# A transformer block with mixture of experts: the last block's rows reach the last four tiles through products instead of a store and gathers

## The chip, the core and the metric

The kernel runs on one core of a Trainium2 chip. The metric is device time in microseconds of one execution, start to end, as the median of several runs. Engine names are those of the profile: PE is TensorE (PEld its weight loads), DVE is VectorE, ACT is ScalarE, POOL is GpSimd, SP is SyncE, which here only issues DMAs.

## The reference

The input is `x` of 32 sequences x 256 steps x 256 features, with one condition vector per sequence. Two layers follow each other:

```python
x = x + attn(cond(x, cond_1024))       # gated input, causal attention of one head over 256 steps
x = x + ffn(cond2(x, cond_1024))       # low-rank conditioned layer, then the block below
```

`ffn` attends over the first axis, of 32, with the 256 steps as its batch (16 heads over 4 key groups), and ends in a mixture of experts over all 8192 tokens:

```python
logits = ln2(h1) @ router_weight                       # 8 experts
top_p, top_i = top_k(softmax(logits), 2)               # 2 experts a token, weights sum to 1
# tokens sorted by expert, at most cap = 2560 a expert; later ones are dropped
fc1 = gelu(einsum('ech,ehf->ecf', xt, moe_w1))         # 256 -> 512
fc2 = einsum('ecf,efh->ech', fc1, moe_w2)              # 512 -> 256
out = h1 + scatter_add(token, fc2 * prob)              # both experts' rows, weighted, back at the token
```

The change lies in the last line: how the experts' rows come back to their tokens. All data are float32.

## The kernel before

**Stages.** By the profile's time the first layer runs up to about 370 us, the attention of the second layer up to about 700 us, and the experts from there to the end. The change is in the last third.

**Experts by blocks.** The (token, expert) pairs are laid out in slots: 256 slots a block, each block of one expert. Block `n` takes four steps. `gather(n)` (L736) brings the 256 tokens' rows from DRAM with two indirect DMAs on POOL's queue. `turn_in(n)` (L753) transposes them on PE and scales them on DVE. `weights(n)` (L744) copies the expert's weights on DVE (L748). `hidden(n)` (L765) and `result(n)` (L778) are the two products on PE, 16 of 128x256 each, with GELU and a copy out of PSUM on ACT. `result` then stores the block's 256 rows to `y_d` in DRAM, from SP.

**Slots of a token.** The routing puts into `yrow[:, j, k]` the slot of each of the 128 tokens of tile `j` (there are 64 tiles, 16 groups of four) for its k-th expert, and into `prob[:, j, k]` its weight, zero where the pair was dropped. Routing is complete before block 20, called `AHEAD`.

**How many blocks.** The number of blocks depends on the data. Three variants of the code from block 20 on are in the program, for 54, 62 and 74 blocks, and a register picks one (`arm`, L1680 on). These inputs take the first, of 54: the profile has 108 gathers `xx<-z_d`, two a block.

**Back to the tokens.** In `experts` (L1617), tile by tile: `fetch_rows(j)` issues two indirect DMAs on POOL's queue (L1633), which gather from `y_d` the rows of the tile's tokens for k = 0 and 1, and for the first tile of a group one load `rs<-res_d` on SP (L1627), the residual rows of the whole group. `combine(j)` does `ot = yg*prob + rs` and `ot = yg*prob + ot` on DVE (L1644), and after the fourth tile stores the group's 512 KB with four DMAs on SP (L1650).

**When a tile may be fetched.** The pairs were laid out so that the slots of early tiles lie in early blocks. `ready[g]` is the number of blocks that must be in `y_d` before group `g` may be gathered; with 54 blocks it is 22, 24, 26, ... 49 (group 13), 51 (group 14), 54 (group 15). In each block from 20 on the loop fetches up to two tiles that are ready, and combines them two blocks later. Group 15, the tiles 60 to 63, needs all 54 blocks, so it is fetched after the loop: first all four `fetch_rows`, then the combines of tiles 58 to 63.

**What sets the order.** The experts' part is under a manual schedule: each engine runs its instructions in the order in which they are written, and so does each engine's DMA queue. An instruction that waits holds up all that is written behind it for the same engine.

Of the kernel before, what the change touches and what calls it, by code (L numbers as in the profile page):

```python
# [9 lines left out]
F32 = mybir.dt.float32  # L10
I32 = mybir.dt.int32
BF16 = mybir.dt.bfloat16
AF = mybir.ActivationFunctionType
ALU = mybir.AluOpType
AX = mybir.AxisListType
PSUM = bass.MemoryType.PSUM
DRAM = bass.MemoryType.DRAM

P = 128
S = 32  # L20
T = 256
D = 256
# [4 lines left out]
NJ = NTOK // P  # L27
NSG = NJ // 4
CAP = int(math.ceil(NTOK * 2 / NE * 1.25))
BLK = 256  # L30
# [7 lines left out]
AHEAD = 20  # L38
# [11 lines left out]
def block_kernel(ctx: ExitStack, tc: tile.TileContext, a: dict, out: bass.AP):  # L50
# [14 lines left out]
    nc = tc.nc  # L65
# [9 lines left out]
    ident = const.tile([P, P], F32, name="ident")  # L75
# [41 lines left out]
    with ExitStack() as c1:  # L117
# [40 lines left out]
        def load_c2w2(f):  # L158
# [7 lines left out]
            out=fac.rearrange("s f o -> s (f o)"), in_=a["c2_b2"].to_broadcast([S, 2 * RANK * D])  # L166
# [9 lines left out]
        base = k1.tile([P, 2, DR], F32, name="base")  # L176
        nc.sync.dma_start(
            out=base[:, :, :D], in_=a["base"].rearrange("(c p) o -> p c o", p=P)
# [13 lines left out]
        for blk in (0, 2):  # L192
            nc.gpsimd.affine_select(
                out=cmask[:, blk, :], in_=cmask[:, blk, :], compare_op=ALU.is_ge,
# [299 lines left out]
        def low_rank(s):  # L494
# [44 lines left out]
            scale_g, pattern=[[1, NSG]], base=1, channel_multiplier=0,  # L539
            allow_small_or_imprecise_dtypes=True,  # L540
# [4 lines left out]
            rev, pattern=[[-1, NE]], base=NE, channel_multiplier=0,  # L545
            allow_small_or_imprecise_dtypes=True,
# [26 lines left out]
        for b in range(4):  # L573
            q = slice(32 * b, 32 * b + 32)
            nc.gpsimd.affine_select(
                out=lows[q], in_=lows[q], compare_op=ALU.is_gt, fill=0.0, base=0,
                pattern=[[0, 4], [1, S]], channel_multiplier=-1,
# [5 lines left out]
            out=lowp, in_=ones, compare_op=ALU.is_gt, fill=0.0, base=0,  # L583
            pattern=[[1, P]], channel_multiplier=-1,
# [4 lines left out]
            icolf, pattern=[[1, P], [0, 8]], base=0, channel_multiplier=0,  # L589
            allow_small_or_imprecise_dtypes=True,  # L590
# [8 lines left out]
            irowf, pattern=[[1, 2 * NB]], base=0, channel_multiplier=0,  # L599
            allow_small_or_imprecise_dtypes=True,  # L600
# [16 lines left out]
        for i in range(2):  # L617
# [4 lines left out]
            prow, pattern=[[0, 1]], base=0, channel_multiplier=1,  # L622
            allow_small_or_imprecise_dtypes=True,
# [22 lines left out]
        for q in range(3):  # L646
            for b in range(4):
                r = SURE * (4 * q + b)
                nc.sync.dma_start(
                    out=rowbitsc[r : r + SURE],  # L650
                    in_=rowbits[32 * b : 32 * b + SURE, PACK * q : PACK * (q + 1)],
# [11 lines left out]
        for b in range(4):  # L663
            q = slice(32 * b, 32 * b + 32)
            for vb in vbd:
                nc.vector.memset(vb[q, :, b, HD:], 1.0)
            nc.gpsimd.affine_select(
                out=tmask[q], in_=tmask[q], compare_op=ALU.is_ge, fill=NEG, base=0,
                pattern=[[0, 2], [-1, S]], channel_multiplier=1,
# [43 lines left out]
    prob = keep.tile([P, NJ, 2], F32, name="prob")  # L713
    gap = keep.tile([P, NJ], F32, name="gap")
    yrow = keep.tile([P, NJ, 2], I32, name="yrow")
# [13 lines left out]
    hts = [ep.tile([P, 4, BLK], F32, name=f"ht{i}") for i in range(2)]  # L729
    yss = [ep.tile([P, 2, D], F32, name=f"ys{i}") for i in range(2)]  # L730
# [3 lines left out]
    xgs, wcs = [], []  # L734

    def gather(n):  # L736
        for h in range(2):
            nc.gpsimd.indirect_dma_start(  # L738
                out=xgs[n % 4][:, h, :], out_offset=None,
                in_=z2_d[: 3 * PACK * P, :] if n < EARLYB else z2_d[:, :],  # L740
                in_offset=bass.IndirectOffsetOnAxis(ap=src_row[:, n, h : h + 1], axis=0),
            )
# [35 lines left out]
    def result(n, ps):  # L778
        we2 = wcs[n % 2][:, 1].rearrange("p (c d) -> p c d", c=4)
        for h in range(2):  # L780
            for f in range(4):
                nc.tensor.matmul(  # L782
                    ps[:, h, :], lhsT=hts[n % 2][:, f, h * P : (h + 1) * P],
                    rhs=we2[:, f, :], start=(f == 0), stop=(f == 3),
                )
        nc.scalar.copy(yss[n % 2], ps)  # L786
        nc.sync.dma_start(
            out=y_d[BLK * n : BLK * (n + 1), :].rearrange("(p h) d -> p h d", h=2),
            in_=yss[n % 2],
        )  # L790
# [529 lines left out]
    out_v = out.rearrange("s (j b) d -> b s j d", b=4)  # L1320
# [3 lines left out]
    p_ys = [pc.tile([P, 2, D], F32, name=f"ps_y{i}") for i in range(2)]  # L1324
    with tc.tile_pool(name="rt", bufs=1) as rt, tc.tile_pool(
        name="rw", bufs=4
# [287 lines left out]
    order.close()  # L1614


    def experts(count, ready, w3):  # L1617

        groups = [{} for _ in range(NSG)]

        def fetch_rows(j):

            g, i = j // 4, j % 4
            v = groups[g]
            if i == 0:
                v["rs"] = w3.tile([P, 4, D], F32, name="rs")
                nc.sync.dma_start(  # L1627
                    out=v["rs"].rearrange("p j d -> p (j d)"), in_=res_d[g]
                )
            upto = ready[g] * BLK  # L1630
            for k in range(2):
                yg = v[i, k] = w3.tile([P, D], F32, name=f"yg{k}", bufs=8)
                nc.gpsimd.indirect_dma_start(  # L1633
                    out=yg, out_offset=None, in_=y_d[:upto, :],
                    in_offset=bass.IndirectOffsetOnAxis(ap=yrow[:, j, k : k + 1], axis=0),
                )

        def combine(j):
            g, i = j // 4, j % 4
            v = groups[g]  # L1640
            if i == 0:
                v["ot"] = w3.tile([P, 4, D], F32, name="ot")
            for k in range(2):
                nc.vector.scalar_tensor_tensor(  # L1644
                    v["ot"][:, i, :], v[i, k], prob[:, j, k : k + 1],
                    v["rs"][:, i, :] if k == 0 else v["ot"][:, i, :], ALU.mult, ALU.add,
                )
            if i == 3:
                for b in range(4):
                    nc.sync.dma_start(  # L1650
                        out=out_v[b, :, 4 * g : 4 * g + 4, :],
                        in_=v["ot"][32 * b : 32 * b + 32],
                    )


        fetched, due = 0, []
        for n in range(AHEAD, count):
            if n + 3 < count:
                gather(n + 3)
            for f2 in range(2):  # L1660
                hidden(n, f2, p_hs[f2])
            if n + 1 < count:
                turn_in(n + 1, p_x)
                weights(n + 1)
            result(n, p_ys[n % 2])
            while due and due[0][0] <= n:
                combine(due.pop(0)[1])
            for _ in range(2):
                if fetched < NJ and ready[fetched // 4] <= n:
                    fetch_rows(fetched)  # L1670
                    due.append((n + 2, fetched))
                    fetched += 1
        while due or fetched < NJ:
            while fetched < NJ and len(due) < 8:
                fetch_rows(fetched)
                due.append((0, fetched))
                fetched += 1
            combine(due.pop(0)[1])

    def arm(count, ready):  # L1680
        with tc.tile_pool(name="w3", bufs=2) as w3, tc.manual_schedule():
            experts(count, ready, w3)

    which = nc.values_load(plan[0:1, 0:1], min_val=0, max_val=len(PLANS) - 1)
    with ExitStack() as elses:
# [60 lines left out]
```

## Time and profile before

| | us |
|---|---|
| runs | 1166.71, 1166.76, 1170.42 |
| median | 1166.76 |
| profiled execution's own time | 1165.57 |
| its span, first to last instruction | 1163.8 |

| engine | busy us | share |
|---|---|---|
| PE | 1075.2 | 92% |
| DVE | 704.8 | 61% |
| POOL | 531.0 | 46% |
| ACT | 392.4 | 34% |

The own time lies 1.8 us over the span. Times inside the profile are us from the span's start. In the profile's lines, `yg<-y_d,yrow` names what is written and what is read, `x4` is a count, and a bracket `[3.62 <-DVE ot L1644]` gives the engine's idle time before the line and what the profile believes ended it. Lines with `SPq` are DMA issues; their time is the issue's, not the transfer's.

### The profile page before, as it was taken

The numbers are of one execution on the slowest core, as the hardware profiler recorded it, in microseconds if no ns is written. First come the engines' busy times: TensorE is split into PE (matmuls) and PEld (weight loads), VectorE is DVE, ScalarE is ACT, GpSimd is POOL, SyncE is SP. The second block draws the span as 40 slices with busy tenths as digits, with TensorE's granted clock in tenths as the row PEclk, the third lists the DMA queues.
The fourth block names the chain that finished last, engine by engine and source line by source line (L and its number), as shares of the span: only waits on it lengthen the run. The fifth ranks groups of instructions, "written<-read, shape, count | busy, mean of one in ns | idle before, by whom it ended". The sixth has DMA issues, their size and how long they took to land.

```text
span 1163.8 us, 17054 instructions
## 1 busy us (share of the span) xinstructions
PE 1075.2 (92%) x5724; PEld 866.3 (74%) x5724; DVE 704.8 (61%) x1784; ACT 392.4 (34%) x942; POOL 531.0 (46%) x781
## 2 busy tenths in 40 slices
PE   8999999999994999999998869997999999999891
PEld 5576888888872777777776648885888888787771
DVE  3554555555561888888888975986222455445452
ACT  2222333333332566666664313210222222222220
POOL 2022222222222466566665545203332777777774
PEclk9999999999997999999999959997999999999996
DMA  9452333333164134254352114101221566665655
GB/s 316 115 148 93 109 114 116 114 115 116 66 155 125 39 111 166 96 182 160 135 180 78 39 64 145 55 37 47 81 73 52 185 203 205 183 204 178 205 182 155
DMA packets 86192, 149.51 MB, mean 128 GB/s; under 512 B 11544, under 2 KB 52144, under 8 KB 85552
## 3 DMA queue, kind: packets, MB, share of 16 engines
q1 hardware_dynamic: 70160, 100.02, 26.5%
q0 software_dynamic: 15936, 48.32, 13.5%
q8 instruction: 47, 0.77, 0.3%
q14 instruction: 49, 0.40, 0.1%
HBM read 90.96 MB, written 57.22 MB: 127 GB/s over the span
## 4 chain that ended last, share of the span: by engine, by line
PE 72%; issue 9%; DMA 8%; DVE 7%; POOL 3%; ACT 1%; SPq 0%; DVEq 0%; POOLq 0%; ACTq 0%
PE ps_y L782 10%; PE ps_h L770 9%; PE p_qkv L858 6%; PE p L502 5%; PE p_z L385 5%; PE p_v L398 5%; PE p_pr L963 4%; PE p_av L929 4%; DMA yg<-y_d,yrow 4%; DMA xx<-z_d,src_row 3%; PE p_sc L888 3%; PE ps_t L917 3%; PE p_s L438 2%; PE p_o L471 2%; PE p_l L413 2%
## 5 line engine op out<-in xcount | busy, mean ns | idle before, releaser
L770 PE MATMUL ps_h<-xt,xx 128*128 128x256 f32 x864 | 197.6, 382 | 0.8 <-DVE xt L760 0.8
L782 PE MATMUL ps_y<-xx,ht 128*128 128x256 f32 x864 | 197.3, 382 | 0.0
L738 POOL DMA_INDIRECT xx<-z_d,src_row x108 | 124.3, 1151 | 149.7 <-issue 78.8
L770 PEld LDWEIGHTS ps_h<-xt,xx 128*128 128x128 f32 x864 | 164.8, 191 | 24.0 <-DVE xt L760 1.2
L782 PEld LDWEIGHTS ps_y<-xx,ht 128*128 128x128 f32 x864 | 161.4, 192 | 20.6 <-ACT ht L774 0.3
L760 DVE TENSOR_SCALAR xt<-ps_xt,ln 128x256 f32<-128x256 f32 x106 | 52.8, 540 | 196.0 <-PE ps_xt L756 196.0
L1633 POOL DMA_INDIRECT yg<-y_d,yrow x128 | 132.1, 1032 | 55.9 <-issue 39.4
L95 POOL TENSOR_SCALAR ve<-mv 128x2 f32<-128x2 f32 (+2 forms) x49 | 10.8, 219 | 237.4 <-DVE mv L103 236.3
L774 ACT ACTIVATE ht<-ps_h 128x512 f32<-128x512 f32 x108 | 64.5, 597 | 136.0 <-PE ps_h L770 134.8
L786 ACT COPY ys<-ps_y 128x512 f32<-128x512 f32 x54 | 31.7, 586 | 213.0 <-PE ps_y L782 182.6
L858 PE MATMUL p_qkv<-wqkv,lnt 128*128 128x384 f32 x256 | 94.7, 494 | 0.0
L908 POOL TENSOR_TENSOR sc<-sc,mx 128x512 f32<-128x512 f32 x64 | 67.9, 1060 | 53.4 <-DVE mx L907 47.5
L929 PEld LDWEIGHTS p_av<-vbd,pt 128*128 128x128 f32 x512 | 68.0, 196 | 27.4 <-ACT pt L922 13.1
L868 ACT COPY vbd<-p_qkv 32x64 f32<-32x64 f32 x256 | 52.7, 206 | 90.2 <-DVE qk L864 87.9
L929 PE MATMUL p_av<-vbd,pt 128*128 128x68 f32 x512 | 67.0, 275 | 8.1 <-ACT pt L922 5.9
L963 PE MATMUL p_pr<-wp,ao 128*128 128x264 f32 x256 | 73.3, 410 | 0.0
L385 PE MATMUL p_z<-yt,m_qk 128*128 128x256 f32 x256 | 68.9, 396 | 0.8 <-ACT yt L370 0.8
L968 POOL TENSOR_TENSOR res<-h,xx 128x256 f32<-128x256 f32 x64 | 43.8, 684 | 54.6 <-DVE h L967 54.4
L748 DVE COPY xx<-wall 128x2048 f32 x54 | 67.4, 1249 | 1.7 <-DMA xx<-z_d,src_row 1.4
L502 PE MATMUL p<-layer,x1t 128*128 128x264 f32 x256 | 66.1, 402 | 2.1 <-ACT x1t L492 1.5
L398 PE MATMUL p_v<-w_vo,yt 128*128 128x256 f32 x256 | 60.6, 379 | 0.0
L502 PEld LDWEIGHTS p<-layer,x1t 128*128 128x128 f32 x256 | 47.1, 194 | 15.7 <-ACT x1t L492 7.4
(302 smaller groups left out, 1874.0 us busy)
## 6 DMA issues: line engine op xcount, KB each, us to landing
xx_d<-o POOLq DMA_DIRECT2D x32, 530.0 KB, 3.5
y_d<-ys SPq DMA_DIRECT2D x54, 256.0 KB
xx<-xx_d SPq DMA_DIRECT2D x13, 1060.0 KB
xt<-in_x_t_dram SPq DMA_DIRECT2D x32, 256.0 KB
xs<-in_x_dram SPq DMA_DIRECT2D x32, 256.0 KB
wall<-in_moe_w_dram SPq DMA_DIRECT2D x16, 512.0 KB
z_d<-h SPq DMA_DIRECT2D x16, 512.0 KB
res_d<-res SPq DMA_DIRECT2D x16, 512.0 KB
```

The costliest lines, as they stand in the source:

```text
L385: nc.tensor.matmul(p_z[:, m, :], lhsT=m_qk[:, c, m * P : (m + 1) * P], rhs=yt[:, c, :], start=(c == 0), stop=(c == 1),)
L398: nc.tensor.matmul(p_v[:, t, :], lhsT=yt[:, c, t * P : (t + 1) * P], rhs=w_vo[:, c, :], start=(c == 0), stop=(c == 1),)
L502: nc.tensor.matmul(p_2, lhsT=v["x1t"][:, c, t * P : (t + 1) * P], rhs=v["layer"][:, c, :], start=(c == 0), stop=(c == 1),)
L738: nc.gpsimd.indirect_dma_start(out=xgs[n % 4][:, h, :], out_offset=None, in_=z2_d[: 3 * PACK * P, :] if n < EARLYB else z2_d[:, :], in_off ...
L748: nc.vector.tensor_copy(wcs[n % 2].rearrange("p a f -> p (a f)"), wall[:, bass.ds(e, 1), :, :].rearrange("p e a f -> p (e a f)"),)
L770: nc.tensor.matmul(ps[:, i, :], lhsT=we1[:, c, f * P : (f + 1) * P], rhs=xts[n % 2][:, c, :], start=(c == 0), stop=(c == 1),)
L782: nc.tensor.matmul(ps[:, h, :], lhsT=hts[n % 2][:, f, h * P : (h + 1) * P], rhs=we2[:, f, :], start=(f == 0), stop=(f == 3),)
L858: nc.tensor.matmul(ps, lhsT=live2[n // 4]["lnt"][:, c, j * P : (j + 1) * P], rhs=wqkv[:, c, :], start=(c == 0), stop=(c == 1),)
L908: nc.gpsimd.tensor_tensor(sc, sc, mx.unsqueeze(2).to_broadcast([P, 16, S]), ALU.subtract)
L929: nc.tensor.matmul(p_a[:, g // 2, :, g % 2, :], lhsT=v["pt"][:, g, :], rhs=vbd[n % 5][:, g], start=True, stop=True,)
L963: nc.tensor.matmul(p_p, lhsT=tiles[n]["ao"][:, gp, :], rhs=wp2[:, gp, :], start=(gp == 0), stop=(gp == 1),)
L1633: nc.gpsimd.indirect_dma_start(out=yg, out_offset=None, in_=y_d[:upto, :], in_offset=bass.IndirectOffsetOnAxis(ap=yrow[:, j, k : k + 1], a ...
```

## The change

For the variants where group 14 is ready before the last block (54 and 62 blocks; not 74), the last block's rows are not stored and not gathered. Group 15 waits for 53 blocks only. For its four tiles:

- Setup, once, ahead of block 20's work: an iota on POOL that numbers the 256 slots of the last block, a float copy of `yrow`, weights `prob_l` that are zero where the slot lies in the last block, and `yrow_l`, the slot clipped to the last row before that block.
- `mark(i)`, in blocks 20 to 23: three DVE instructions make a matrix of 128 tokens x 256 slots, with the weight where the token's slot is, and zero elsewhere.
- `turn_marks(i)`, in blocks 21 to 24: two transposes on PE and a copy on ACT turn it into `own`, slots by tokens.
- `result_alone`, in place of the last `result`: the same 16 products, copied out of PSUM by halves; then eight products of 128x256, `own` by the block's rows, into `p_own`. No store to `y_d`.
- `fetch_rows` of group 15 moves into the loop, at the last block, behind the combines that are due there; from block 51 on up to four tiles are fetched in a block, so that tiles 56 to 59 are all fetched at 51 and combined at 53.
- `combine` of group 15 has a third DVE instruction a tile, which adds `p_own`; its stores go out after every second tile, 64 KB each, alternately from SP and ACT.

```diff
@@ -1614,9 +1614,71 @@
     order.close()
 
 
-    def experts(count, ready, w3):
+    def experts(count, ready, w3, w3p):
+
+
 
         groups = [{} for _ in range(NSG)]
+        last, end = count - 1, NJ - 4
+        alone = w3p is not None
+        if alone:
+            assert ready[NSG - 2] <= last
+            ready = [*ready[:-1], last]
+            own = w3.tile([P, 2, 4, P], F32, name="own", bufs=1)
+            pos = w3.tile([P, 2, P], F32, name="pos", bufs=1)
+            nc.gpsimd.iota(
+                pos, pattern=[[1, 2], [2, P]], base=last * BLK, channel_multiplier=0,
+                allow_small_or_imprecise_dtypes=True,
+            )
+            at_row = w3.tile([P, 4, 2], F32, name="at_row", bufs=1)
+            nc.vector.tensor_copy(at_row, yrow[:, end:, :])
+
+            prob_l = w3.tile([P, 4, 2], F32, name="prob_l", bufs=1)
+            nc.vector.scalar_tensor_tensor(
+                prob_l, at_row, float(last * BLK), prob[:, end:, :], ALU.is_lt, ALU.mult
+            )
+            yrow_l = w3.tile([P, 4, 2], I32, name="yrow_l", bufs=1)
+            nc.vector.tensor_scalar(yrow_l, at_row, float(last * BLK - 1), None, ALU.min)
+            marks = {}
+
+        def mark(i):
+
+            ms = []
+            for k in range(2):
+                m = w3.tile([P, 2, P], F32, name=f"mark{k}")
+                nc.vector.tensor_scalar(
+                    m, pos, at_row[:, i, k : k + 1], prob[:, end + i, k : k + 1],
+                    ALU.is_equal, ALU.mult,
+                )
+                ms.append(m)
+            nc.vector.tensor_tensor(ms[0], *ms, ALU.add)
+            marks[i] = ms[0]
+
+        def turn_marks(i):
+            ps = w3p.tile([P, 2, P], F32, name="p_mark")
+            for h in range(2):
+                nc.tensor.transpose(ps[:, h, :], marks[i][:, h, :], ident)
+            nc.scalar.copy(own[:, :, i, :], ps)
+
+        def result_alone():
+            n = last
+            ps, we2 = p_ys[n % 2], wcs[n % 2][:, 1].rearrange("p (c d) -> p c d", c=4)
+            ys = yss[n % 2]
+            for h in range(2):
+                for f in range(4):
+                    nc.tensor.matmul(
+                        ps[:, h, :], lhsT=hts[n % 2][:, f, h * P : (h + 1) * P],
+                        rhs=we2[:, f, :], start=(f == 0), stop=(f == 3),
+                    )
+                nc.scalar.copy(ys[:, h, :], ps[:, h, :])
+            p_own = w3p.tile([P, 4, D], F32, name="p_own")
+            for i in range(4):
+                for h in range(2):
+                    nc.tensor.matmul(
+                        p_own[:, i, :], lhsT=own[:, h, i, :], rhs=ys[:, h, :],
+                        start=(h == 0), stop=(h == 1),
+                    )
+            return p_own
 
         def fetch_rows(j):
 
@@ -1632,7 +1694,11 @@
                 yg = v[i, k] = w3.tile([P, D], F32, name=f"yg{k}", bufs=8)
                 nc.gpsimd.indirect_dma_start(
                     out=yg, out_offset=None, in_=y_d[:upto, :],
-                    in_offset=bass.IndirectOffsetOnAxis(ap=yrow[:, j, k : k + 1], axis=0),
+                    in_offset=bass.IndirectOffsetOnAxis(
+                        ap=yrow_l[:, i, k : k + 1] if alone and j >= end
+                        else yrow[:, j, k : k + 1],
+                        axis=0,
+                    ),
                 )
 
         def combine(j):
@@ -1641,15 +1707,22 @@
             if i == 0:
                 v["ot"] = w3.tile([P, 4, D], F32, name="ot")
             for k in range(2):
+                w = prob_l[:, i] if alone and j >= end else prob[:, j]
                 nc.vector.scalar_tensor_tensor(
-                    v["ot"][:, i, :], v[i, k], prob[:, j, k : k + 1],
+                    v["ot"][:, i, :], v[i, k], w[:, k : k + 1],
                     v["rs"][:, i, :] if k == 0 else v["ot"][:, i, :], ALU.mult, ALU.add,
                 )
-            if i == 3:
+            n = 4
+            if alone and j >= end:
+                nc.vector.tensor_tensor(
+                    v["ot"][:, i, :], p_own[:, i, :], v["ot"][:, i, :], ALU.add
+                )
+                n = 2
+            if (i + 1) % n == 0:
                 for b in range(4):
-                    nc.sync.dma_start(
-                        out=out_v[b, :, 4 * g : 4 * g + 4, :],
-                        in_=v["ot"][32 * b : 32 * b + 32],
+                    (nc.scalar if n == 2 and b % 2 else nc.sync).dma_start(
+                        out=out_v[b, :, 4 * g + i + 1 - n : 4 * g + i + 1, :],
+                        in_=v["ot"][32 * b : 32 * b + 32, i + 1 - n : i + 1],
                     )
 
 
@@ -1662,10 +1735,17 @@
             if n + 1 < count:
                 turn_in(n + 1, p_x)
                 weights(n + 1)
-            result(n, p_ys[n % 2])
+            if alone and AHEAD < n <= AHEAD + 4:
+                turn_marks(n - AHEAD - 1)
+            if alone and n < AHEAD + 4:
+                mark(n - AHEAD)
+            if alone and n == last:
+                p_own = result_alone()
+            else:
+                result(n, p_ys[n % 2])
             while due and due[0][0] <= n:
                 combine(due.pop(0)[1])
-            for _ in range(2):
+            for _ in range(4 if alone and n >= ready[NSG - 2] else 2):
                 if fetched < NJ and ready[fetched // 4] <= n:
                     fetch_rows(fetched)
                     due.append((n + 2, fetched))
@@ -1678,8 +1758,12 @@
             combine(due.pop(0)[1])
 
     def arm(count, ready):
-        with tc.tile_pool(name="w3", bufs=2) as w3, tc.manual_schedule():
-            experts(count, ready, w3)
+        with tc.tile_pool(name="w3", bufs=2) as w3, ExitStack() as st:
+            w3p = None
+            if ready[NSG - 2] < count:
+                w3p = st.enter_context(tc.tile_pool(name="w3p", bufs=1, space=PSUM))
+            st.enter_context(tc.manual_schedule())
+            experts(count, ready, w3, w3p)
 
     which = nc.values_load(plan[0:1, 0:1], min_val=0, max_val=len(PLANS) - 1)
     with ExitStack() as elses:
```

## The prediction

> **What bounds the kernel now.** I read the page first (engines, slices, the chain), then the groups of GpSimd, then GpSimd's timeline of the last third, then the timeline of all engines over the last 45 us, and last the DMA share of the tail. The page alone misleads:
>
> ```profile
> PE 1075.2 (92%) x5724; PEld 866.3 (74%) x5724; DVE 704.8 (61%) x1784; ACT 392.4 (34%) x942; POOL 531.0 (46%) x781
> PE 72%; issue 9%; DMA 8%; DVE 7%; POOL 3%; ACT 1%; SPq 0%; DVEq 0%; POOLq 0%; ACTq 0%
> ```
>
> TensorE is busy 92% of the span and GpSimd 46%, but that is an average. The groups of GpSimd alone, from 899.8 to 1141 us (blocks 23 to 53):
>
> ```profile
> L1633 POOL DMA_INDIRECT yg<-y_d,yrow x119 | 123.6, 1038 | 38.6 <-issue 26.4 <-DVE ot L1644 4.3 <-DMA xx<-z_d,src_row 4.0
> L738 POOL DMA_INDIRECT xx<-z_d,src_row x56 | 64.4, 1151 | 17.1 <-issue 11.3 <-DMA yg<-y_d,yrow 2.7 <-PE ps_h L770 1.8
> ```
>
> After the `|` stand busy us, mean ns, and idle before it. 175 gathers with 55.7 us before them: in the timeline, from the gather at 899.88 on, every gap is 0.30 to 0.32 us, the queue's own step, until the last gather of that stretch ends at 1140.92. So GpSimd is never waiting in this stage; it issues a gather every 1.25 us, and TensorE, whose block takes 7.35 us undisturbed, waits for `xx` (gaps of 0.9 to 2.4 us before L756). Six gathers a block are 7.5 us, more when one is stretched. The tail of the timeline of all engines (start, duration, and in brackets idle before):
>
> ```profile
> 1136.25 3.77 PE L782 MATMUL ps_y<-xx,ht 128*128 128x256 f32 x16
> ...
> 1139.75 1.17 POOL L1633 DMA_INDIRECT yg<-y_d,yrow  x1 [0.31 <-issue]
> 1140.10 0.59 ACT L786 COPY ys<-ps_y 128x512 f32<-128x512 f32 x1 [2.99 <-PE ps_y L782]
> 1140.71 0.34 SPq L787 DMA_DIRECT2D y_d<-ys  x1
> 1141.10 0.54 SPq L1627 DMA_DIRECT2D rs<-res_d  x1
> ...
> 1143.20 0.48 DVE L1644 SCALAR_TENSOR_TENSOR ot<-yg,prob,ot 128x256 f32<-128x256 f32 x1 [1.02 <-DMA yg<-y_d,yrow]
> 1143.71 14.68 SPq L1650 DMA_DIRECT2D out_dram<-ot  x8
> 1144.54 0.94 POOL L1633 DMA_INDIRECT yg<-y_d,yrow  x1 [3.62 <-DVE ot L1644]
> ...
> 1147.94 0.48 DVE L1644 SCALAR_TENSOR_TENSOR ot<-yg,prob,rs 128x256 f32<-128x256 f32 x1 [4.26 <-DMA out_dram<-ot]
> ...
> 1153.29 0.95 POOL L1633 DMA_INDIRECT yg<-y_d,yrow  x1 [0.31 <-DVE ot L1644]
> 1156.11 0.48 DVE L1644 SCALAR_TENSOR_TENSOR ot<-yg,prob,ot 128x256 f32<-128x256 f32 x1 [0.76 <-DMA yg<-y_d,yrow]
> ```
>
> The reader sees here what the last block's store costs: GpSimd is done with tile 59's gathers at 1140.92 and stands still for 3.62 us until 1144.54 (named after DVE, long done: the store issued at 1140.71 is what it waits for). Eight gathers follow, 1.25 us apart; each is used about 2.8 us after its start (1153.29 to 1156.11). Then the stores, in windows of the tail:
>
> ```profile
> 1156.60:1157.40 0.80, 0.00 (x0) 0.00 (x0) 0.00 (x0) 0.00 (x0) 0.00 (x0) 0.50 0.04 10
> 1157.40:1159.80 2.40, 0.00 (x0) 0.00 (x0) 0.00 (x0) 0.00 (x0) 0.00 (x0) 0.50 0.89 222
> 1159.80:1163.80 4.00, 0.00 (x0) 0.00 (x0) 0.00 (x0) 0.00 (x0) 0.00 (x0) 0.50 0.01 4
> ```
>
> The last two columns are DMA share and GB/s: 0.8 us of latency, 2.4 us for 512 KB, 4.0 us of completion and end of program. So the last sum ends at 1156.59 and the span 7.2 us later.
>
> **The change, part by part.** The sum is made on the span of 1163.8 us.
>
> *The gathers of tiles 60 to 63.* They no longer need block 53, only block 52, whose store was issued at 1133.65; the last one took 3.8 us from issue to the gather behind it, so it has landed by 1137.5. But GpSimd's order is unchanged (53's rows, tiles 56 to 59, tiles 60 to 63), and it is busy to 1140.92. So the first gather starts at 1141.2 instead of 1144.54: 3.3 us, not the whole 16 us from TensorE's end to the last sum. The last one starts at 1150.0 and is usable at 1152.8.
>
> *The load of `rs` for the last group.* This is what I expect to come late next. Before, SP issued it at 1141.10, ahead of group 14's stores. Now tiles 56 to 59 are combined inside the loop at n=53, ahead of `fetch_rows(60)`, so on SP the four stores of group 14 stand ahead of it, and they wait for the combine of tile 59, which ends at 1143.68. Four issues take 2.2 us (SP rows L1650 x4), so the load goes out at 1145.9. Its landing R isn't in the trace. From below: the page has 530 KB landing 3.5 us after issue (`xx_d<-o`), so 1149.4. From above: the same load was used 6.8 us after issue (1141.10 to 1147.94), so 1152.7. By bytes: 1.05 MB of stores and load plus gathers at 0.105 MB/us, on engines that moved 268 GB/s from 1142 to 1148, need 6.4 us from 1144.5: 1150.9. I take 1151.0. All eight first sums and adds queue behind it on DVE.
>
> *DVE.* Four tiles now need 12 instructions: two back-to-back sums take 0.90 us (1122.92 to 1123.82), and the add from PSUM is like L506 and L967, 0.40 to 0.43 us. 4 x (0.90+0.43) = 5.3 us after R: 1156.3, against 1156.59. That is -0.3 us, between 1154.7 (-1.9) and 1158.0 (+1.4). If `rs` were not late, the last gather would decide: 1152.8+0.48+0.43 = 1153.7.
>
> *The stores.* The last four move 256 KB, not 512: 2.4 us becomes 1.2, and two of the four issues of 0.44 us move to ACT, which has nothing behind them. -1.2 us, between -1.6 and 0 (if ACT's first DMA here is slow). One more queue to wait for at the end: +0.1.
>
> *Products.* 8 on TensorE at 3.46/16 us each are 1.7 us, behind two copies (ACT rows: 0.27 us for 136 columns, 0.59 for 512). They end by about 1142.3; first use is past R. Hidden by 9 us; had DVE no other wait they would still be earlier than tile 60's second gather. The removed store of 256 KB frees nothing that is late.
>
> *Marks and their transposes, blocks 20 to 24.* Two transposes are half of 0.44 us. TensorE limits only up to block 21's store, which starts GpSimd's stretch, so one pair counts: +0.2 us; the other three pairs fall where TensorE's results lie about 4 us ahead of GpSimd. ACT's four copies (0.27 to 0.59 us) lie in gaps of over 1 us. DVE's marks, three instructions of 0.31 (L1526) to 0.54 us (L760) a tile, fit the 5.2 us in which DVE idles before each L760. The iota (0.35 us for 148 columns, so some 0.6) falls in GpSimd's gaps of 4.5 us before 881; uncovered it would cost itself.
>
> But DVE can stretch a gather:
>
> ```profile
> 1130.42 1.38 POOL L1633 DMA_INDIRECT yg<-y_d,yrow  x1 [0.30 <-DVE xt L760]
> 1130.45 1.23 DVE L748 COPY xx<-wall 128x2048 f32 x1
> ```
>
> 1.38 us instead of 0.95 beside L748; the longest is 1.99, so at most 1.04 each. At 0.945 each, 175 gathers would be 165.4 us; they took 188.0, so 22.6 us is lost this way, 0.8 us for each of about 28 copies. Marks 0 and 1 come while GpSimd is idle, marks 2 and 3 (near 898.6 and 906) beside its stretch. Between 0 and one full stretch, 1.04; I take +0.5.
>
> [...]
>
> Sum: -0.3 -1.2 +0.1 +0.2 +0.5 = -0.7 us. Span 1163.1. The profiled execution's own time, 1165.57, lies 1.2 us under the median 1166.76; from the median, 1166.0. Ends: -1.9-1.6+0.1+0.2+0 = -3.2 and +1.4+0+0.1+0.2+1.04 = +2.7, so 1163.6 to 1169.5.
>
> **The rivals.** *`rs` in time.* If the load is in by 1148 the gathers decide, DVE ends at 1153.7 (-2.9), and with -1.2+0.1+0.2+0.5 that is -3.3; without the lockout, and with the stores at their lower end, -4.2: 1162.6. For it: only one landing is bounded above. Against: 2 us from issue to landing, half of the page's 3.5.
>
> *The full wait goes.* If GpSimd were idle when block 52 lands, all eight gathers would pass during block 53 and the end would be TensorE's: 1140.0+0.5+1.7+1.3+6.1 = 1149.6, so 1152.6 by the median. Against it stands every 0.30 us gap.
>
> [...] Marks and later transposes move DVE's L748 against the gathers; in this stage each us lost on GpSimd is lost at the end. It decides when the loss per copy rises from 0.8 to about 0.95 (28 x 0.15 = 4.2); at the longest row's 1.04 it is +6.7, with the rest +5.5: 1172. For it: the loop has no slack and stretches vary between 0.43 and 1.04. Against: the marks touch two blocks only.
>
> **How the numbers follow.** A difference of under 0.3% (3.5 us) is about what a measurement of this kernel can't tell from none: three runs spread over 3.7 us. The forecast is no change, 0.63, at 1166.0. Faster by more: `rs` in time 0.15, the full wait 0.03, unknown 0.02. Slower: 0.17. The range reaches to the `rs` rival on one side, 1162.6, and to the bound 1169.5 on the other; beyond lie the full wait, a part of the first rival and most of the slower one, about 0.2.
>
> **What would show it.** In the profile after: no gap over 0.4 us on GpSimd between tile 59's and tile 60's gathers (right) or a gap of 3 us (wrong). SP's `rs` load issued after four stores, near 1146, and DVE standing still from about 1144 to 1151 before its first sum of tile 60, with twelve instructions back to back behind it: right. DVE waiting for `yg` instead: the first rival. `p_own` done near 1142, used 9 us later. L738 and L1633 means above 1.15 and 1.04 us: the slower one. I am wrong altogether if GpSimd shows idle gaps in blocks 40 to 53.

## The result, and the profile after

Nothing that can be measured. The kernel after took 1166.99 us in the median of 20 runs (1162.26 to 1170.74), the kernel before beside it 1166.32 (20 runs, 1162.21 to 1174.46): ratio 1.0000, 95% interval 0.9984 to 1.0016. A second set of runs gave 1165.91 against 1165.63: 1.0008, 0.9990 to 1.0027. The forecast was 1166.0, no change.

The page after, engines and chain:

```profile
PE 1076.1 (93%) x5748; PEld 867.6 (75%) x5748; DVE 709.8 (61%) x1803; ACT 393.7 (34%) x947; POOL 532.9 (46%) x782
PE 76%; DVE 8%; issue 7%; DMA 6%; POOL 1%; ACT 1%; SPq 0%; DVEq 0%; POOLq 0%; ACTq 0%
```

The engines' totals hardly move; on the chain TensorE has 76% for 72% and DVE 8% for 7%, and DMA, GpSimd and "issue" two less each. The groups of GpSimd after, from 896 to 1140 us (busy us, mean ns, idle before):

```profile
L1695 POOL DMA_INDIRECT yg<-y_d,yrow x119 | 125.5, 1055 | 37.5 <-issue 23.5 <-DMA xx<-z_d,src_row 4.6 <-DVE ot L1711 4.3
L738 POOL DMA_INDIRECT xx<-z_d,src_row x56 | 63.2, 1129 | 17.1 <-issue 9.1 <-PE ps_y L782 3.0 <-DMA yg<-y_d,yrow 2.4
```

The same 175 gathers, the same 0.30 to 0.31 us between them, nearly the same stretched means: GpSimd's queue is as full as before. The tail after, all engines (start, duration, idle before):

```profile
1137.14 1.05 POOL L1695 DMA_INDIRECT yg<-y_d,yrow  x1 [0.30 <-DMA yg<-y_d,yrow]
...
1137.41 3.92 PE L1677 MATMUL p_own<-ys,own 128*128 128x256 f32 x16
...
1138.49 1.13 POOL L1695 DMA_INDIRECT yg<-y_d,yrow_l  x1 [0.30 <-DMA yg<-y_d,yrow]
...
1140.60 0.48 DVE L1711 SCALAR_TENSOR_TENSOR ot<-yg,prob,ot 128x256 f32<-128x256 f32 x1 [0.19 <-DMA yg<-y_d,yrow]
...
1142.93 0.45 SPq L1689 DMA_DIRECT2D rs<-res_d  x1
...
1147.41 0.94 POOL L1695 DMA_INDIRECT yg<-y_d,yrow_l  x1 [0.30 <-issue]
1149.49 0.48 DVE L1711 SCALAR_TENSOR_TENSOR ot<-yg,prob_l,rs 128x256 f32<-128x256 f32 x1 [8.41 <-DMA rs<-res_d]
...
1150.61 0.42 DVE L1717 TENSOR_TENSOR ot<-p_own,ot 128x256 f32<-128x256 f32 x1
...
1154.72 0.42 DVE L1717 TENSOR_TENSOR ot<-p_own,ot 128x256 f32<-128x256 f32 x1
```

The 3.62 us gap between tile 59's last gather and tile 60's first is gone (0.30). In its place DVE stands 8.41 us for `rs`, whose load SP could issue only at 1142.93, behind group 14's stores, which waited for the sum at 1140.60. The first gather of tile 60 had been issued 11.0 us before its first use. The trace's record of DMA packets agrees with the name on DVE's row: the load is 128 packets of 4 KB, the last of them ends at 1148.99, 0.50 us before the sum, and tile 60's first gather had all its packets in by about 1142. `p_own` is done at 1141.33 and used at 1150.61. The stores' end in windows (the last two columns are DMA share and GB/s):

```profile
1155.20:1156.00 0.80, 0.00 (x0) 0.00 (x0) 0.00 (x0) 0.00 (x0) 0.00 (x0) 0.50 0.06 14
1156.00:1157.30 1.30, 0.00 (x0) 0.00 (x0) 0.00 (x0) 0.00 (x0) 0.00 (x0) 0.50 0.80 212
1157.30:1160.90 3.60, 0.00 (x0) 0.00 (x0) 0.00 (x0) 0.00 (x0) 0.00 (x0) 0.50 0.02 7
```

The transfer takes 1.3 us instead of 2.4.

Between fixed points of the trace, from block 20's first product on, in the two profiles that each kernel has (us):

| stretch | before | before, again | after | after, again | predicted change |
|---|---|---|---|---|---|
| block 20's first product to the second `yg` gather | 22.18 | 22.14 | 23.49 | 23.93 | +0.2 |
| to the start of tile 59's last gather | 239.87 | 242.46 | 240.75 | 244.13 | +0.5 |
| to the end of the last sum | 16.84 | 15.90 | 18.00 | 17.49 | -0.3 |
| to the end of the span | 7.21 | 7.70 | 5.76 | 5.54 | -1.1 |
| sum | 286.10 | 288.20 | 288.00 | 291.09 | -0.7 |

What lies ahead of block 20 varied from 871.7 to 877.7 us in these four and isn't the change's. The last row's pairs differ by +1.9 and +2.9 us; the second row varies by 2.6 and 3.4 us between two profiles of one kernel, more than between the kernels; the others agree within 1 us.

### The profile page after: what moved, and what is told of

It reads as the page before. It is cut to its first block, busy times and chain, and to the rows that moved or that the text cites. A ratio compares the mean times of both kernels' runs of the same rounds, so it can differ in the third digit from the quotient of the medians.

```text
span 1160.9 us, 17134 instructions
## 1 busy us (share of the span) xinstructions
PE 1076.1 (93%) x5748; PEld 867.6 (75%) x5748; DVE 709.8 (61%) x1803; ACT 393.7 (34%) x947; POOL 532.9 (46%) x782
## 4 chain that ended last, share of the span: by engine, by line
PE 76%; DVE 8%; issue 7%; DMA 6%; POOL 1%; ACT 1%; SPq 0%; DVEq 0%; POOLq 0%; ACTq 0%
PE ps_y L782 12%; PE ps_h L770 11%; PE p_qkv L858 6%; PE p L502 5%; PE p_z L385 5%; PE p_v L398 5%; PE p_pr L963 4%; PE p_av L929 4%; PE p_sc L888 3%; DMA xx<-z_d,src_row 3%; PE ps_t L917 3%; PE p_s L438 2%; PE p_o L471 2%; PE p_l L413 2%; DMA yg<-y_d,yrow 2%
## 5 line engine op out<-in xcount | busy, mean ns | idle before, releaser
L782 PEld LDWEIGHTS ps_y<-xx,ht 128*128 128x128 f32 x848 | 159.9, 193 | 20.5
L1695 POOL DMA_INDIRECT yg<-y_d,yrow x120 | 127.6, 1063 | 50.4 <-issue 23.5
L748 DVE COPY xx<-wall 128x2048 f32 x54 | 66.8, 1238 | 1.5 <-DMA xx<-z_d,src_row 1.4
L858 PEld LDWEIGHTS p_qkv<-wqkv,lnt 128*128 128x128 f32 x256 | 44.4, 193 | 18.4 <-ACT lnt L822 1.1
```

The costliest lines, as they stand in the source:

```text
L748: nc.vector.tensor_copy(wcs[n % 2].rearrange("p a f -> p (a f)"), wall[:, bass.ds(e, 1), :, :].rearrange("p e a f -> p (e a f)"),)
L782: nc.tensor.matmul(ps[:, h, :], lhsT=hts[n % 2][:, f, h * P : (h + 1) * P], rhs=we2[:, f, :], start=(f == 0), stop=(f == 3),)
L858: nc.tensor.matmul(ps, lhsT=live2[n // 4]["lnt"][:, c, j * P : (j + 1) * P], rhs=wqkv[:, c, :], start=(c == 0), stop=(c == 1),)
L1695: nc.gpsimd.indirect_dma_start(out=yg, out_offset=None, in_=y_d[:upto, :], in_offset=bass.IndirectOffsetOnAxis(ap=yrow_l[:, i, k : k + 1] ...
```

## The experiments

**The theory.** From block 23 to 53 GpSimd's queue is the limit, because DVE's weights copy (L748) stretches its gathers (1.38 us for 0.95 in the kernel before, 22.6 us over 175 of them). While that queue is late, taking away block 53's store can only move the last gathers by the 3 us that they waited beyond the queue; and the residual load, now behind group 14's stores, takes those 3 us back. **Rivals**: the change is worth nothing in itself, wherever it runs; the gathers land late, and not the load; the marks cost what the tail gains.

Four sets of runs beside the kernel before. In the sets e, f and h every kernel, the kernel before too, took 60 to 80 us longer (kernel before: 1246.40, 1245.38 and 1226.78 us), and every profile taken in them shows it in the expert stage, so times are compared within a set only. The kernel before without edits was timed in these sets but not profiled. The "tail" is from the start of the last block's second product on TensorE (the first `ps_y` row of block 53) to the end of the span. "Stretch" is what the 175 gathers up to tile 59's last took over 0.945 us each; "gaps" the sum of GpSimd's gaps of over 0.5 us among them and the gather ahead.

| set, kernel | median us | ratio to before, 95% | stretch | gaps | tail |
|---|---|---|---|---|---|
| before | 1166.32 | | 22.6 | 2.6 | 27.6 |
| after | 1166.99 | 1.0000, 0.9984 to 1.0016 | 23.4 | 1.5 | 27.9 |
| g before | (one run: 1161.73) | | 25.0 | 2.6 | 27.7 |
| g after | 1165.91 | 1.0008, 0.9990 to 1.0027 | 26.9 | 2.0 | 26.6 |
| e after, `rs` first | 1234.51 | 0.9908, 0.9868 to 0.9947 | 16.2 | 83.0 | 20.3 |
| e before, copy on ACT | 1241.25 | 0.9973, 0.9937 to 1.0009 | 1.2 | 93.5 | 27.8 |
| e after, copy on ACT | 1233.96 | 0.9891, 0.9837 to 0.9946 | 1.4 | 95.9 | 22.5 |
| e after, no marks | 1236.48 | 0.9920, 0.9885 to 0.9956 | 15.6 | 78.3 | 19.7 |
| f after, `rs` first | 1233.96 | 0.9886, 0.9852 to 0.9920 | 16.0 | 81.8 | 20.1 |
| f before, copy on ACT | 1236.19 | 0.9958, 0.9924 to 0.9992 | 0.9 | 96.6 | 28.8 |
| f after, copy on ACT | 1230.38 | 0.9873, 0.9835 to 0.9912 | 0.8 | 99.5 | 20.8 |
| f after, both | 1231.69 | 0.9900, 0.9859 to 0.9940 | 1.4 | 95.8 | 21.5 |
| h after, `rs` first | 1234.54 | none | 16.9 | 81.6 | 20.2 |
| h after, both | 1228.12 | none | 3.3 | 90.0 | 21.2 |

In set h the 11 runs of the kernel before lay between 1194 and 1244 us, so no ratio can be read from it. The tails of its two kernels can; their medians, 1234.54 and 1228.12, don't lie under the kernel before's 1226.78.

### The weights copy on ACT, with and without the change

In both kernels, ahead of the DVE copy:

```diff
+        if n > AHEAD:
+            nc.scalar.load(areg, eid[0:1, at_ : at_ + 1], bass_reorder=False)
+            e = nc.scalar.snap(areg, min_val=0, max_val=NE - 1)
+            nc.scalar.copy(wcs[n % 2]..., wall[:, bass.ds(e, 1), :, :]...)
+            return
```

The kernel before with it, expected in set e:

> The kernel before, with the copy of the expert's weights (L748) on ACT instead of DVE for blocks 21 to 53. Theory (GpSimd limits this stage, and DVE's copy stretches its gathers by 22.7 us in all): no gather over 1.2 us, the block falls to TensorE's 7.35 us, result(53) ends near 250 us after block 20's first product instead of 262, and the time falls by about 12 us. Rival (TensorE or the DMAs limit, GpSimd only keeps pace): gathers are short, but the time falls by under 2 us.

in set f:

> The kernel before with one edit: from block 21 on the copy of an expert's weights runs on ACT instead of DVE. Theory (in blocks 23 to 53 GpSimd's queue is the limit and the DVE copy costs it 22.6 us of stretched gathers): the stretches fall from 22.7 us to under 3, and TensorE, at 7.35 us a block, becomes the limit of this stage; 8 to 15 us sooner, 1152 to 1159. Rival (the stretches are hidden, TensorE limits): within 2 us of 1166.

The kernel after with it, set e:

> The changed kernel with the same copy on ACT for blocks 21 to 53. Theory (the change was worth only 3.3 us of GpSimd's wait because GpSimd ran late): with GpSimd ahead of TensorE, the gathers of tiles 60 to 63 run during block 53, and the change is worth 6 to 8 us against the kernel before with the copy on ACT; about 19 us under the kernel before. Rival (the rs load or the extra DVE work eats the gain in any case): within 2 us of the kernel before with the copy on ACT.

set f:

> The changed kernel with the same edit, the copy of the weights on ACT from block 21 on. Theory: with GpSimd no longer late at block 52, the gathers of the last four tiles go out in block 53 beside TensorE's last products, and the change is worth what it was meant to be: 5 to 9 us under the kernel before with the same edit, 1144 to 1152. Rival (the change is worth nothing in itself): the same as the kernel before with the copy on ACT.

Measured: the stretches are gone, as the theory wants. GpSimd's groups in the kernel after with the copy on ACT (set f, 900 to 1212 us):

```profile
L1704 POOL DMA_INDIRECT yg<-y_d,yrow x119 | 113.1, 951 | 127.5 <-DVE ot L1720 67.0 <-issue 44.0 <-DMA y_d<-ys 15.0
L739 POOL DMA_INDIRECT xx<-z_d,src_row x56 | 53.0, 947 | 20.8 <-issue 14.0 <-remote 4.1 <-PE ps_h L779 2.7
```

951 and 947 ns a gather, against 1055 and 1129 in the kernel after of the first set, and in set f itself 0.8 us of stretch against 16.0 with the copy on DVE, with the sums, the scaling and (in blocks 20 to 23) the marks still on DVE: the copy on DVE is what stretched them; by what means, no run shows. But the 8 to 15 us of time did not come: 0.3% (an interval that holds 1) and 0.4% for the kernel before. In these sets GpSimd wasn't the limit, with gaps of 78 to 100 us in all kernels, whichever engine copied. What freeing the queue is worth where it is full is therefore not measured.

These sets show something else: the change where GpSimd has time. The two kernels of a set differ by the change alone. Before, with the copy on ACT (set f, tail):

```profile
1206.37 3.72 PE L791 MATMUL ps_y<-xx,ht 128*128 128x256 f32 x16 [0.41 <-ACT ht L783]
...
1210.78 0.34 SPq L796 DMA_DIRECT2D y_d<-ys  x1
...
1215.54 0.94 POOL L1642 DMA_INDIRECT yg<-y_d,yrow  x1 [12.11 <-issue]
...
1227.11 0.48 DVE L1653 SCALAR_TENSOR_TENSOR ot<-yg,prob,ot 128x256 f32<-128x256 f32 x1 [0.77 <-DMA yg<-y_d,yrow]
```

After, with the copy on ACT (set f, tail):

```profile
1214.35 0.32 SPq L796 DMA_DIRECT2D y_d<-ys  x1
...
1214.88 1.99 PE L1678 MATMUL ps_y<-xx,ht 128*128 128x256 f32 x8 [0.43 <-ACT ht L783]
...
1217.15 0.95 POOL L1704 DMA_INDIRECT yg<-y_d,yrow_l  x1 [5.19 <-DMA y_d<-ys]
...
1218.65 0.43 SPq L1698 DMA_DIRECT2D rs<-res_d  x1
...
1224.35 0.48 DVE L1720 SCALAR_TENSOR_TENSOR ot<-yg,prob_l,rs 128x256 f32<-128x256 f32 x1 [9.73 <-issue]
...
1229.57 0.42 DVE L1726 TENSOR_TENSOR ot<-p_own,ot 128x256 f32<-128x256 f32 x1
```

Before, tile 60's first gather starts 9.2 us after TensorE's last product begins: 4.4 for the product and its copy, 4.8 for the store. After, it starts 2.3 us after, held only by block 52's store, and the span ends 20.8 us after instead of 28.8 (set e: 22.5 and 27.8). In the medians that is 5.8 us (0.9873 against 0.9958, intervals apart) and 7.3 in set e (0.9891 against 0.9973, intervals that overlap a little). So the first rival falls: the change in itself is worth 5 to 8 us at the tail, and it shows where GpSimd is idle when block 52's rows land. The load is late here too: its last packet ends at 1223.83, 0.52 us before the first sum at 1224.35. But in set f it costs nothing more, since the last gather's packets end at 1228.51 and its sum and the add behind it then need until about 1229.9; the last sum ends at 1229.99.

### The change as it is, and the kernel before, once more

> The changed kernel as it is, beside the kernel before, on the chip on which the expert stage takes some 70 us longer in every kernel and GpSimd therefore stands idle in each block. Theory (the change's gain is eaten by GpSimd's late queue): here GpSimd isn't late at block 52, the gathers of the last four tiles start during block 53, and the change is worth about what it is with the weights copied on ACT on this chip, 0.7 to 1.1% under before; in the profile, from the start of the last block's second product to the end of the span, 20 to 22 us instead of 27.9. Rival (the change is worth nothing wherever it runs): within 0.3% of before, and 27 to 29 us. If the chip is one on which the stage isn't longer: within 0.3% of before.

> The kernel before, for its profile on the same chip. Theory: GpSimd has gaps of several us in blocks 23 to 53 and is idle when block 53's store is issued, so that store and the eight gathers stand in full: 27 to 30 us from the start of the last block's second product to the end. Rival: the same 20 to 22 us as the changed kernel.

This set turned out as the first: the kernel before at 1165.63, GpSimd without gaps, the change at 1.0008. It is the case that the first text's last sentence names, and its tail, 26.6 against 27.7, is far from the 20 to 22 us of an idle GpSimd, as in the first set. The longer stage did not come back for this pair, so the two kernels without further edits were never run side by side in it.

### The residual load first

```diff
+            if alone and n == last - 1:
+                load_rs(NSG - 1)          # group 15's load, at block 52
             for _ in range(4 if alone and n >= ready[NSG - 2] else 2):
```

`load_rs` holds the lines of the load that stood in `fetch_rows`, which now skips it for this group.

> The changed kernel, with group 15's load of rs issued from SP at block 52, ahead of group 14's four stores. Theory (the load queued behind the stores is what came late): DVE no longer stands 8.4 us before tile 60; it follows the gathers, and its last instruction ends about 3.7 us after the start of the last gather instead of 7.7. From the start of tile 59's last gather to the end of the span 19.8 us instead of 23.8; the time falls by 4 us. Rival (the gathers' landing or the load of the DMA engines sets the end): under 1 us of change, DVE waiting for yg instead of rs.

> The changed kernel with one edit: the load of the last group's residual rows is issued on SP at block 52, ahead of group 14's stores. Theory (GpSimd's queue sets when the last gathers go, and behind them the late residual load sets when the sums start): the first sum of tile 60 no longer waits for the load but for its gather, DVE ends about 3.5 us sooner after tile 59's last gather than the changed kernel (18.0 there, about 14.5 here), from that gather to the end about 20 us instead of 23.8; time about 1163, 0.3% under before. Rival (the gathers land late, the load isn't what is waited for): under 1 us gained, 1166 to 1167.

> The changed kernel with one edit: the load of the last group's residual rows is issued on SP at block 52, ahead of group 14's stores. On a chip where the kernel before takes about 1166 us: theory (with GpSimd's queue full the residual load is the last thing the sums wait for): DVE's first sum of tile 60 comes 3 to 4 us after its gather instead of 11.0, the last gather decides, and from tile 59's last gather to the end 19.5 to 21 us instead of 23.8; 1162 to 1163.5. Rival (the gathers themselves land late): under 1 us gained, 1165 to 1167. Where the stage is some 70 us longer: 1.0 to 1.2% under before, as measured there.

It gained nothing that shows over its nearest neighbour: tails of 20.3 and 20.1 us, against 19.7 in the kernel without marks, which has the load behind the stores. The reason lies in the sets: where GpSimd has gaps, group 14's tiles are summed early, and SP issues the load soon in any case, 1.7 us after TensorE's last product begins in the kernel without marks, where the first and the repeated profile of the kernel after have 9.9 and 9.4. The edit had 2 us to move, not the 5 of the full queue. What it did show (set f):

```profile
1216.17 0.44 SPq L1685 DMA_DIRECT2D rs<-res_d  x1
1216.62 0.94 POOL L1696 DMA_INDIRECT yg<-y_d,yrow_l  x1 [11.14 <-DMA y_d<-ys]
...
1221.64 0.49 DVE L1712 SCALAR_TENSOR_TENSOR ot<-yg,prob_l,rs 128x256 f32<-128x256 f32 x1 [6.84 <-DMA rs<-res_d]
```

The row names the load, but the load's last packet ended at 1220.52, 4.35 us after its issue; the packets of tile 60's first gather end at 1221.14, 0.50 us before the sum. So DVE waited for the gather, as the theory said. In set e the row names the gather, and the packets agree: the load's end at 1215.48, 4.72 us after issue, the gather's at 1215.84, the sum starts at 1216.28. Behind the four stores, in the two profiles of the kernel after, the load's last packet came 6.06 and 5.35 us after issue. But the gather beside the early load took 4.5 us from start to last packet in both, for 3.0 and 2.7 in the kernel before, and DVE then stood 2.36 and 2.75 us more between tile 60's first and second sum, for which the profile names no releaser.

Whether issuing the load earlier pays where GpSimd's queue is full wasn't measured: no set with this edit was of that kind. Two estimates from the rows: in the kernel after the last sum ends 7.7 and 7.3 us after the last gather starts, in the two kernels with the load first 5.4 and 5.2, so some 2 us; and in the kernel after the last gather's packets end at 1150.26 and 1156.69 (in the repeated profile), 4.9 and 4.8 us before the end of the last sum, of which a sum and an add behind the gather need about 1.4, so at most 3.5 us.

### The marks left out

```diff
-            if alone and AHEAD < n <= AHEAD + 4:
-                turn_marks(n - AHEAD - 1)
-            if alone and n < AHEAD + 4:
-                mark(n - AHEAD)
+            if alone and n == AHEAD:
+                nc.gpsimd.memset(own, 0.0)
```

> The changed kernel without the marks and their transposes and copies (own is zero: what the last block gives to the last four tiles is left out). Theory (marks 2 and 3 stretch gathers and the first pair of transposes delays block 21's store): from block 20's first product to the end 286.3 us instead of 288.0, of which 0.2 us are the transposes. Rival (the marks are hidden, and the 2 us are the scatter of where copies and gathers meet): the same 288 within 0.5 us, with the sum of stretches still above 23 us.

The median, 1236.48, lies 2.0 and 2.5 us above those of its set with marks (1234.51 and 1233.96), so in time they cost nothing that this set can show. Their place is seen in the trace. From block 20's first product to block 22's it is 14.69 us in every profile without marks and 14.91 in every one with them: the pair of transposes, 0.22 us. The first `yg` gather starts 18.6 us after block 20's first product in the kernel before (18.63, 18.58) and with its copy on ACT (18.57, 18.58), 18.4 without marks; with marks and the copy on DVE it is 19.9, 20.4, 20.5, 18.6 and 20.3 (after, again, and the load first in sets e, f and h); with marks and the copy on ACT 18.6 in all four. So in four profiles of nine with marks the stage starts 1.3 to 1.9 us late.

What holds the gather there is not the marks' own work. It waits for block 21's store (in the kernel after 12.89 us idle before the gather, `<-DMA y_d<-ys`), issued 15.8 us after block 20's first product in every profile with marks. The DMA packets around that store, in the kernel after (888.5 to 892.0 us) and, below, in the load-first kernel of set f (889.3 to 892.3 us); after a queue stand packets, MB and the share of the DMA engines' time:

```profile
q1 hardware_dynamic: 144, 0.26, 19.9%
q8 instruction: 1, 0.02, 2.3%
```

```profile
q1 hardware_dynamic: 144, 0.26, 22.6%
```

In the kernel after, the one packet of 16 KB on the queue that the profile names `q8 instruction` ran beside the store, from 16.35 to 17.63 us after block 20's first product. The store's last eight packets of 2 KB start between 17.63 and 18.46, and the last one ends at 18.54; without the q8 packet, in set f, at 17.38. The same stands in the other three late profiles (last packets at 18.91 to 19.09). In the ten others the q8 packet is over before the store's first packet, or there is none near it. That the store's packets waited for it is read from these times alone. With the copy on DVE and no marks the q8 packet begins about 0.8 us ahead of the store's issue in all three profiles; with marks 0.6 to 1.4 us behind it in four, and 1.3 ahead in the fifth, of the same load-first kernel that has it behind in sets e and h. So the marks may well move the q8 packet, but that is inferred from where it lies, and chance has a part in it.

### Both edits

The kernel after with the load first and the copy on ACT:

> The changed kernel with both edits: residual load first, weights copied on ACT. Theory: the end is then set by TensorE's last products or by the last gather, 2 to 4 us under the changed kernel with the copy on ACT alone, 1142 to 1149. Rival (the load isn't late once the gathers are early): the same as with the copy on ACT alone.

> The changed kernel with two edits: the residual load first, and the copy of the weights on ACT instead of DVE from block 21 on. Where the kernel before takes about 1166 us: theory (the DVE copy stretches GpSimd's gathers and so sets this stage's length): the stretches fall from 23.5 us to under 3, TensorE at 7.35 us a block becomes the limit, GpSimd shows gaps, and the last block's gathers run beside its products; 1142 to 1150. Rival (the stretches are hidden behind TensorE or ACT becomes the limit): within 2 us of the changed kernel with the load first alone. Where the stage is some 70 us longer: 0.9 to 1.3% under before, as measured there.

0.9900 in set f, no less than either edit alone (0.9886 and 0.9873; the intervals overlap), with tails of 21.5 and 21.2. Both texts expected the gain of a full queue set free; there was none to free. What the second named for the longer stage, 0.9 to 1.3% under the kernel before, can't be read from set h. All kernels with the change in the sets e and f are 0.8 to 1.3% under the kernel before, but none with a further edit was measured beside a kernel before of 1166 us, so a version that beats both kernels isn't shown.

## Why the prediction was right

**The bound: right.** GpSimd's queue stayed without gaps to tile 59's last gather, in both profiles of the kernel after, and the first gather of tile 60 moved by the few us of its gap (4.79 and 3.59 us after tile 59's last before, 1.35 and 1.42 after). "The full wait goes" failed by the very condition it was given, GpSimd idle when block 52 lands; the sets e and f, where the condition holds, show its gain in kind, 5 to 8 us of the 14 named.

**The residual load: right in kind, the mis-sized term.** It went out behind four stores and became what DVE waits for, as said. The landing R was taken at 5.1 us after issue by bytes, between 3.5 and 6.8; its last packet came after 6.1 and 5.4 and it was used after 6.6 and 6.0. Up to the use that is +1.5 and +0.9, of which 0.5 and 0.6 us lie between the last packet and the sum, a step that the text gave to the gathers and not to this load. The `rs` rival ("in time") is out.

**DVE:** twelve instructions back to back, 5.65 us from first start to last end, for 5.3. From tile 59's last gather to the last sum +1.2 and +1.6 (each profile after against the matching one before) instead of -0.3. In the first pair the load's term makes most of it; in the second the before profile is also 0.9 us shorter here than its first one. The upper end was +1.4.

**Stores:** -1.5 and -2.2 us from last sum to end, for -1.1 (-1.2 and +0.1). No row shows the +0.1, for one more queue to wait for, by itself.

**Products:** 1.7 us was half of what they take. The trace has two rows for each product (`p_own` x16 for eight calls, as `ps_y` x16 for the eight of `result`), and the text priced eight rows: 3.92 us. They stayed hidden, as said, but the 14 us of "the full wait goes" were some 2 us too many by it.

**Marks:** the transposes 0.22 for +0.2. What they add to GpSimd's stretch was put at +0.5; whether the stretch grew (+0.9 and +1.7) is less than its own spread. At the stage's start stand +1.3 and +1.8, of which 0.2 are the transposes and the rest the late landing of block 21's store beside the 16 KB packet of q8 (last packet at 18.54 for 17.38), a term that the text did not have. It is over the bound of +1.04 plus 0.2 that the text gave for marks and transposes. The range's lower end, 1162.6, leaves out this +0.5 under the name of a lockout: no run shows a lockout; they show gathers stretched beside DVE's copy, 23.4 and 26.9 us in all after, for 22.6 and 25.0 before.

**The sum:** -0.7 predicted, about +2 in the profiles from block 20 on (+1.9 and +2.9), +0.67 and +0.28 in the medians. The terms of the tail cancel nearly as said: about -3 for the gathers, taken back by the load, and -1.8 for the stores against the start of the stage. That the median came within 1 us of 1166.0 is in part luck: the store's late landing was not in the sum, and the long stretch alone varies by 2.6 to 3.4 us between two profiles of one kernel.

**The slower outcome,** a loss that grows beside every copy, did not come: GpSimd's means after are 1055 and 1129 ns, for 1038 and 1151 before; repeated, 1060 and 1179 for 1044 and 1181. `yg` is a little above the text's mark of 1.04 us, `xx` about its mark of 1.15 in both kernels, and the medians don't follow.

## What to carry to other kernels

A wait at the end of a kernel is worth only what it lasts beyond the queue that stands in front of it: ask first whether the engine that will do the freed work is idle at that moment. When a step is moved ahead in the program, look at what each DMA queue issued between its old and its new place; here one load slipped 5 us behind four stores and took over the wait. And a change that gains nothing beside one limit can gain where that limit is absent, as here in the sets with the longer stage; whether an edit that lifts the limit brings the same wasn't measured, so the two should be tried together. Last, a row that comes late need not owe it to the change: read first which DMA packets ran beside what it waits for.

## What the runs showed of the hardware that was not expected

- The copy of 128x2048 floats takes 1.25 us on DVE and 1.90 on ACT, and on ACT it costs GpSimd's gathers next to nothing: 0.8 to 3.3 us of stretch over 175 gathers, for 22.6 to 26.9 beside the DVE copy where the queue is full, and 16 to 17 in the sets e, f and h.
- Beside a packet of 16 KB on the queue `q8 instruction`, of 1.29 us in the kernel after, the last eight packets of a 256 KB store started when it had ended, and the store's last packet came 1.2 us later than in the load-first kernel of set f without it (18.54 for 17.38 us after block 20's first product).
- The packets of a 512 KB load ended 4.35 and 4.72 us after its issue with no store of the group before it ahead on its queue, 6.06 and 5.35 behind four of them.
- In the sets e, f and h ACT and DVE stood still ahead of work on TensorE's results, again and again, with `remote` as the releaser that the profile names: in the kernel before with the copy on ACT (set f), from 900 to 1200 us, DVE 139.0 us before L769, in 16 waits of up to 24.8. The transposes here end at 905.7:

```profile
905.06 0.60 PE L765 MATMUL ps_xt<-ident,xx 128*128 128x128 f32 x4
...
910.10 0.60 ACT L783 ACTIVATE ht<-ps_h 128x512 f32<-128x512 f32 x1 [6.54 <-remote]
...
922.73 0.60 ACT L783 ACTIVATE ht<-ps_h 128x512 f32<-128x512 f32 x1 [12.03 <-remote]
```

  The stage was about 70 us longer there; up to block 20 the times are the same: the first `yg` gather starts between 890.3 and 896.5 us in all profiles. The granted clock of TensorE fell too. From 900 to 960 us, in the kernel before and, below, in the one of set f with the copy on ACT (busy us of PE, PEld, DVE, ACT and POOL, then clock, DMA share, GB/s):

```profile
900.00:960.00 60.00, 60.00 (x295) 52.86 (x294) 29.92 (x52) 14.82 (x25) 46.90 (x44) 1.00 0.60 189
900.00:960.00 60.00, 41.38 (x180) 34.46 (x179) 13.78 (x30) 18.10 (x21) 29.16 (x32) 0.84 0.41 124
```

  From 880 us to its last product TensorE stands still for 57 to 67 us in the eight profiles of the sets e and f, and its clock is at 0.50 for 55 to 72 us; in the four of the first set and of g it is 10 to 13 and 0 to 7 us. In each of the eight the first pause comes before the first stretch at half clock (in set f 905.66 and 910.08), so the clock does not begin it. What does isn't known.
